# The row of f_j by two small transfers through DRAM in place of four transposes

## The chip, the cores and the metric

The kernel runs on one core of a Trainium2 chip. The metric is the device time of one execution in microseconds (us); the kernel before takes 2719.64 us in the median of three runs (2719.47 to 2719.93). A core has five engines with a queue of instructions each: TensorE (PE, matrix products and transposes; its weight loads are shown as PEld), VectorE (DVE), ScalarE (ACT), GpSimd (POOL) and SyncE (SP, which here only issues transfers). Each works through its own queue in order.

## The reference, cut to what matters

There are 128 graphs of 128 nodes with 256 features, in float32. One gated graph layer comes first, three graph attention layers follow; each is added to its input and normalised.

```python
# layer 0, three steps:  m = h @ weight[i];  aggr = A.T @ m;  h = gru_cell(aggr, h)
#   r, z = sigmoid(i + h);  n = tanh(i_n + r * h_n);  h = (1 - z) * n + z * h
x = layernorm(x + gated(x, adj, ...))
# layers 1, 2, 3:
Wh = x @ W.T
f_i, f_j = Wh @ a1, Wh @ a2
e = f_i[:, :, None] + f_j[:, None, :]
e = where(e > 0, e, 0.2 * e);  e = where(adj == 0, -large, e)
x = layernorm(x + softmax(e, axis=2) @ Wh)
```

The change is about `f_j[:, None, :]`: f_j is one number for each node, and each row i of the scores needs all 128 of them side by side.

## The kernel before, in words

**Tiling.** Nodes lie on the 128 partitions. Graphs go in 32 groups of four (`G = 4`), so that a tile is 128 x 512 (four graphs x 128) or 128 x 1024 (four graphs x 256 features). Each group has two phases: `gru`, the gated layer in three steps, and `gat`, three attention layers.

**The gated phase.** A step aggregates with the adjacency (L498), then multiplies in a two-by-two block scheme with seven products where eight are usual: `product` (L446) on PE writes to PSUM "gate" banks, `add` (L451) on DVE joins parts, ACT applies tanh (L524, L553), DVE and GpSimd form the new state (L540 to L563), and PE transposes it (L579). In the last step the group's x, loaded once more (L569), is added (L582).

**The attention phase.** The scores need f_i and f_j, each a product-sum of a node's features with a vector; L605 makes eight of them on DVE per layer (four graphs for f_j first, then four for f_i), each writing the product itself to a junk tile `fx`. f_j then stands in one column, one node per partition. To get it as a row on all partitions, PE transposes the column, broadcast to 128 x 128, once for each graph (L614), into a PSUM bank. L619 on DVE adds the mask to that row and takes the row's maximum; ACT adds f_i and applies the slope (L623), and takes exp (L640); PE transposes the result (L647), multiplies it with the features (L663) and with the weights (L674); DVE scales and adds the residual (L680). `layernorm` squares on ACT (L389), takes the root on GpSimd (L392, L396) and scales on ACT (L402), from the tile `y` into another tile `xn`.

**What sets the order.** The program is written out in full as a list of operations with what they read and write, and class `Plan` orders them before anything is built. It plays the operations against its own clock: each has an assumed duration for each engine that could do it (for instance 440 ns for four transposes), a result can be used by another engine after `LATENCY` of the engine that made it (4000 ns for a transfer from SP), plus `lag` where an operation states one, and plus `MARGIN` (500 ns) before PE may use it. Among what is ready, the older group goes first; for the last four groups (`LAST = 4`) the stage counts instead, so that these four advance side by side. An operation may start only if a slot is free for each tile that it begins to fill: `pools` gives the number of slots for each kind (26 of "k2", 2 KB per partition; 19 of "k4", 4 KB; 3 PSUM "bank"s and 5 "gate"s), and `own` keeps some back for the oldest group. `port=BOTH` says that DVE and GpSimd may not run it beside each other's such operation. Each engine then runs its instructions in the order found, whatever the real times are; only semaphores hold an instruction back.

**Transfers.** SP issues them in plan order in one queue: `xs` (x of the group, L478), `adj_i` (adjacency as int32, L479), `y` (x again, L569) and the output (L687), each once per group. The int32 adjacency is turned into `am` (float 0 or 1, L483), and later into the additive mask (L570).

Of the kernel before, what the change touches and what calls it, by code (L numbers as in the profile page):

```python
# [23 lines left out]
FAR = -5.0 * 2.0 ** 97  # L24
# [23 lines left out]
class Plan:  # L48
# [2 lines left out]

    LATENCY = {"PE": 250, "ACT": 220, "DVE": 200, "POOL": 250, "SP": 4000}

    MARGIN = 500

# [140 lines left out]
def adj_resnorm_kernel(  # L198
# [14 lines left out]
    nc = tc.nc  # L213
    B = x.shape[0]
    NG = B // G
    LAST = 4

    consts = ctx.enter_context(tc.tile_pool(name="consts", bufs=1))
    work = ctx.enter_context(tc.tile_pool(name="work", bufs=1))
    psum = ctx.enter_context(tc.tile_pool(name="psum", bufs=1, space=bass.MemoryType.PSUM))  # L220


    pools = {"gru": 4, "xs": 2, "adj": 2, "am": 5, "k2": 26, "k4": 19, "fx": 2, "f": 3, "mv": 4, "st": 6, "v": 16,
             "gate": 5, "bank": 3}
    own = ({"k2": 8, "k4": 5, "gate": 2, "v": 5, "fx": 0, "st": 0}, {"k2": 4, "k4": 2, "v": 5, "fx": 0, "st": 0})
    floats = {"gru": 0, "k4": 1024, "xs": 1024, "fx": 256, "f": 8, "mv": 8, "st": 6, "v": 4}
# [3 lines left out]
    slots = {t: [(psum if t in ("gate", "bank") else work).tile([P, w], I32 if t == "adj" else F32, name=f"{t}{i}")  # L230
                 for i in range(n)] for t, (n, w) in tags.items() if w}

    def T(b):
        if b.at is None:
            width = 1
            for s in b.shape:
                width *= s
            at = slots[b.tag][b.slot][:, 0:width]
            if len(b.shape) == 2:
                at = at.rearrange("p (a b) -> p a b", b=b.shape[-1])  # L240
            elif len(b.shape) == 3:
                at = at.rearrange("p (a b c) -> p a b c", b=b.shape[-2], c=b.shape[-1])
            b.at = at
        return b.at

    def bank():
        return Buf("bank", GN)
# [7 lines left out]
    ident = consts.tile([P, P], F32)  # L255
# [111 lines left out]
            res.append(dst)  # L367
        return res

    def layernorm(y, total, dst, prio):  # L370

        rstd, ve, shift = Buf("v", G), Buf("v", G), Buf("v", G)
        if total is None:
            mv = Buf("mv", G, 2)
            for b in range(G):
                st = Buf("st", 6)
                plan.op({"DVE": 400}, lambda e, b=b, st=st: nc.vector.bn_stats(T(st), T(y)[:, b, :]),
                        reads=[(y, b)], writes=[st], prio=prio)
                plan.op({"DVE": 95}, lambda e, b=b, st=st: nc.vector.bn_aggr(T(mv)[:, b, :], T(st)),
                        reads=[st], writes=[(mv, b)], prio=prio)  # L380
            plan.op({"POOL": 229}, lambda e: nc.gpsimd.tensor_scalar(T(ve), T(mv)[:, :, 1], EPS, None, op0=ALU.add),
                    reads=[(mv, b) for b in range(G)], writes=[ve], prio=prio)
            less, keys = (lambda: T(mv)[:, :, 0]), [(mv, b) for b in range(G)]
        else:
            mean, ss = Buf("v", G), Buf("v", G)
            plan.op({"DVE": 100}, lambda e: nc.vector.tensor_scalar(T(mean), T(total), -1.0 / D, None, op0=ALU.mult),  # L386
                    reads=[(total, b) for b in range(G)], writes=[mean], prio=prio)
            for b in range(G):
                plan.op({"ACT": 490}, lambda e, b=b: nc.scalar.activation(  # L389
                    T(dst)[:, b, :], T(y)[:, b, :], AF.Square, bias=T(mean)[:, b:b + 1], accum_out=T(ss)[:, b:b + 1]),  # L390
                    reads=[(y, b), mean], writes=[(dst, b), (ss, b)], prio=prio)
            plan.op({"POOL": 229}, lambda e: nc.gpsimd.tensor_scalar(  # L392
                T(ve), T(ss), 1.0 / D, EPS, op0=ALU.mult, op1=ALU.add),
                reads=[(ss, b) for b in range(G)], writes=[ve], prio=prio)
            less, keys = (lambda: T(mean)), [mean]
        plan.op({"POOL": 1035}, lambda e: nc.gpsimd.tensor_tensor(T(rstd), T(ve), neghalf, ALU.pow),  # L396
                reads=[ve], writes=[rstd], prio=prio)
        plan.op({"DVE": 100}, lambda e: nc.vector.scalar_tensor_tensor(  # L398
            T(shift), less(), -1.0 if total is None else 1.0, T(rstd), op0=ALU.mult, op1=ALU.mult),
            reads=keys + [rstd], writes=[shift], prio=prio)  # L400
        for b in range(G):
            plan.op({"ACT": 500}, lambda e, b=b: nc.scalar.activation(  # L402
                T(dst)[:, b, :], T(y)[:, b, :], AF.Identity, bias=T(shift)[:, b:b + 1], scale=T(rstd)[:, b:b + 1]),
                reads=[(y, b), shift, rstd], writes=[(dst, b)], prio=prio)

    def sums(ms, prio):

# [63 lines left out]

    def gru(g, stage):

        xs, adj_i, am = Buf("xs", G, D), Buf("adj", G, P), Buf("am", G, P)
        prio = stage(g, 0)
        turn = Buf("gru")
        x_g = x[g * G:(g + 1) * G].rearrange("b n d -> n b d")
        plan.op({"SP": 60}, lambda e: nc.sync.dma_start(T(xs), x_g), writes=[xs], prio=prio)  # L478
        plan.op({"SP": 60}, lambda e: nc.sync.dma_start(T(adj_i), adj[g * G:(g + 1) * G].rearrange("b s t -> s b t")),  # L479
                writes=[adj_i], prio=prio)  # L480
        if g == 0:
            hidden_weights(prio)
        plan.op({"DVE": 417}, lambda e: nc.vector.tensor_scalar(T(am), T(adj_i), 0, None, op0=ALU.not_equal),  # L483
                reads=[adj_i], writes=[am, turn], prio=prio, port=BOTH)
        hT = transposed(xs, lambda b, c: T(xs)[:, b, c * P:(c + 1) * P], prio)
        h = None
        for i in range(STEPS):
            prio = stage(g, i)
            if g == 0:
                input_weights(i, prio)  # L490
            agg = []
            for c in range(KC):
                b_, a_ = bank(), Buf("k2", GN)
# [23 lines left out]
            nn = strassen([(2, (h_in,)), (2, (a_in,))], halves, prio)  # L517
            hT2 = []
            for c in range(KC):

                o, v, d = rz[c], nn[c], Buf("k2", GN)
# [44 lines left out]
                hT2.append(d)  # L566
            if last:
                y = Buf("k4", G, D)
                plan.op({"SP": 60}, lambda e: nc.sync.dma_start(T(y), x_g), reads=[agg[0]], writes=[y], prio=prio)  # L569
                plan.op({"DVE": 417}, lambda e: nc.vector.tensor_scalar(  # L570
                    T(am), T(am), 0.0, FAR, op0=ALU.is_equal, op1=ALU.mult), reads=[am], writes=[am], prio=prio, port=BOTH)
            else:
                h2 = [Buf("k2", G, P) for c in range(KC)]
# [17 lines left out]
        x1 = Buf("k4", G, D)  # L591
        layernorm(y, None, x1, prio)
        return x1, am

    def gat(g, xc, no, stage):

        for l in range(3):
# [9 lines left out]
                        accum_out=T(f)[:, b, h:h + 1]), reads=[(xc, b), (wa, l)], writes=[fx, (f, 2 * b + h)], prio=prio, port=BOTH)  # L607
            e_, pT, y = Buf("k2", G, P), Buf("k2", G, P), Buf("k4", G, D)
            top, nmax, den, rden, total = Buf("v", G), Buf("v", G), Buf("v", G), Buf("v", G), Buf("v", G)
            b_ = bank()  # L610

            def fn(e, b_=b_, f=f):
                for b in range(G):
                    nc.tensor.transpose(T(b_)[:, b * P:(b + 1) * P],  # L614
                                        T(f)[:, b, 1:2].to_broadcast([P, P]), ident)
            plan.op({"PE": 440}, fn, reads=[(f, 2 * b + 1) for b in range(G)], writes=[b_], prio=prio)

            for b in range(G):
                plan.op({"DVE": 215}, lambda e, b_=b_, b=b, e_=e_, top=top: nc.vector.tensor_tensor_reduce(  # L619
                    T(e_)[:, b, :], T(b_)[:, b * P:(b + 1) * P], T(no)[:, b, :], 1.0, 3 * FAR, ALU.add, ALU.max,  # L620
                    T(top)[:, b:b + 1]), reads=[b_, no], writes=[(e_, b), (top, b)], prio=prio)
            for b in range(G):
                plan.op({"ACT": 285}, lambda e, b=b, f=f, e_=e_: nc.scalar.activation(  # L623
                    T(e_)[:, b, :], T(e_)[:, b, :], AF.Prelu, bias=T(f)[:, b, 0:1], alpha=SLOPE),
# [43 lines left out]
            for b0 in range(0, G, 2):  # L668
# [9 lines left out]
                for b in (b0, b0 + 1):  # L678
# [5 lines left out]
            xn = Buf("k4", G, D)  # L684
            layernorm(y, total, xn, prio)
            xc = xn
# [57 lines left out]
```

## Time and profile before

| | |
|---|---|
| time, median of 3 | 2719.64 us (2719.47 to 2719.93) |
| span of the profiled run | 2716.7 us |
| PE / weight loads / DVE / ACT / GpSimd busy | 98 / 87 / 75 / 65 / 22% |
| L614, four transposes per layer and group | 384 transposes |
| L619, scores from the PSUM row | 384, 284 ns each on DVE |
| L605, sums for f | 768, 436 ns each on DVE |
| DMA packets, bytes | 70106, 65.39 MB |

How to read it: durations overlap, [...] so what an instruction costs its engine is the distance between two starts. A float32 product is recorded on PE as two MATMUL records, a transpose as one. The line of digits gives 40 equal slices of the span in tenths. "a <- b" in a wait means that a sat idle until b released it.

### The profile page before, as it was taken

Reading aid. Unit: us, or ns where it says so; the run is one execution under the profiler, and the core shown is the slowest. Engines: PE = TensorE matmul, PEld = TensorE weight load, DVE = VectorE, ACT = ScalarE, POOL = GpSimd, SP = SyncE. Lnnn points to the kernel's source line nnn. Section 1 sums busy time; section 2 is a strip of 40 time slices with the busy share of each in tenths; the row PEclk is TensorE's granted clock in tenths of the full one; section 3 lists DMA queues with packets and bytes.
Section 4 is the critical chain, followed back from the end, with each engine's and each line's share of the span. In section 5 each row is a group of like instructions: output and inputs, shape, how many; then the busy total and the mean of one; then the engine's idle time right before and its main releaser. Section 6 shows DMA issues by size and latency. Waiting matters only on the chain.

```text
span 2716.7 us, 42471 instructions
## 1 busy us (share of the span) xinstructions
PE 2660.0 (98%) x14536; PEld 2366.2 (87%) x14536; DVE 2026.1 (75%) x6206; ACT 1760.2 (65%) x4632; POOL 593.0 (22%) x738
## 2 busy tenths in 40 slices
PE   7999999999999999999999999999999999999987
PEld 6888889888888888888888888988988888888875
DVE  4677777787787776777876777877777877776696
ACT  3566666666666666666767666666676666665577
POOL 1013222211131222122221222212222312222021
PEclk9999999999999999999999999999999999999999
DMA  3001000000010100001000000100000000000000
GB/s 120 9 20 36 28 5 24 28 28 20 13 33 12 36 20 20 16 20 36 20 28 28 9 28 20 36 20 20 17 20 28 28 24 21 9 9 27 13 1 32
DMA packets 70106, 65.39 MB, mean 24 GB/s; under 512 B 2688, under 2 KB 68224, under 8 KB 69888
## 3 DMA queue, kind: packets, MB, share of 16 engines
q1 hardware_dynamic: 67584, 58.73, 7.1%
q10 hardware_dynamic: 2304, 3.95, 0.4%
q8 instruction: 114, 1.87, 0.3%
q14 instruction: 104, 0.85, 0.1%
HBM read 45.89 MB, written 16.78 MB: 23 GB/s over the span
## 4 chain that ended last, share of the span: by engine, by line
PE 86%; DVE 8%; ACT 3%; issue 1%; DMA 1%; POOL 0%; POOLq 0%; ACTq 0%; SPq 0%; DVEq 0%
PE gate L446 58%; PE bank L674 10%; PE bank L663 6%; PE bank L498 5%; PE bank L579 3%; DVE fx L605 2%; PE bank L647 1%; DVE k L451 1%; PE bank L614 1%; ACT k L402 1%; ACT k L389 1%; DVE k L680 1%; DVE k L286 1%; PE bank L333 1%; DVE k L540 1%
## 5 line engine op out<-in xcount | busy, mean ns | idle before, releaser
L446 PE MATMUL gate<-k,whs 128*128 128x256 f32 x4032 | 1202.2, 380 | 3.0 <-ACT k L513 2.2
L446 PE MATMUL gate<-k,wcs 128*128 128x256 f32 x4032 | 1199.2, 379 | 0.0
L446 PEld LDWEIGHTS gate<-k,wcs 128*128 128x128 f32 x4032 | 766.1, 190 | 104.0
L446 PEld LDWEIGHTS gate<-k,whs 128*128 128x128 f32 x4032 | 728.5, 190 | 86.2 <-ACT k L513 3.4
L451 DVE TENSOR_TENSOR k<-gate,k 128x512 f32<-128x512 f32 x576 | 390.4, 686 | 264.3 <-PE gate L446 220.9
L284 ACT COPY k<-bank 128x512 f32<-128x512 f32 (+1 forms) x459 | 262.3, 583 | 191.7 <-PE bank L579 62.7
L674 PE MATMUL bank<-gwT,k 128*128 128x256 f32 x1536 | 352.6, 382 | 5.0 <-DVE k L286 3.5
L416 POOL TENSOR_TENSOR k<-k,k 128x256 f32<-128x256 f32 x302 | 248.9, 841 | 402.0 <-DVE k L563 133.9
L674 PEld LDWEIGHTS bank<-gwT,k 128*128 128x128 f32 x1536 | 290.6, 191 | 49.7 <-DVE k L286 8.6
L605 DVE SCALAR_TENSOR_TENSOR fx<-k,wa 128x256 f32<-128x256 f32 x768 | 290.3, 436 | 51.2 <-ACT k L402 49.4
L389 ACT ACTIVATE k<-k,v 128x256 f32<-128x256 f32 x384 | 190.3, 498 | 210.6 <-DVE v L386 210.2
L402 ACT ACTIVATE k<-k,v,v 128x256 f32<-128x256 f32 x512 | 263.7, 593 | 54.7 <-DVE v L398 54.4
L524 ACT ACTIVATE k<-k,brz 128x512 f32<-128x512 f32 (+1 forms) x384 | 226.1, 619 | 80.6 <-DVE k L451 80.2
L680 DVE SCALAR_TENSOR_TENSOR k<-bank,v,k 128x256 f32<-128x256 f32 x384 | 169.9, 480 | 119.9 <-PE bank L674 119.3
L506 ACT COPY k<-gate 128x512 f32<-128x512 f32 x288 | 164.7, 580 | 109.8 <-PE gate L446 108.6
L553 ACT ACTIVATE k<-k,bi 128x512 f32<-128x512 f32 x192 | 137.8, 722 | 108.5 <-DVE k L550 71.1
L663 PEld LDWEIGHTS bank<-k,k 128*128 128x128 f32 x1536 | 185.9, 192 | 14.2 <-DVE k L286 5.3
L663 PE MATMUL bank<-k,k 128*128 128x128 f32 x1536 | 188.2, 275 | 7.8 <-DVE k L286 4.7
L558 POOL TENSOR_TENSOR k<-k,k 128x512 f32<-128x512 f32 x78 | 103.3, 1327 | 412.3 <-ACT k L553 406.1
L286 DVE COPY k<-bank 128x512 f32<-128x512 f32 x225 | 152.9, 685 | 49.3 <-PE bank L579 17.4
L392 POOL TENSOR_SCALAR v<-v 128x4 f32<-128x4 f32 x96 | 20.5, 214 | 773.4 <-ACT k L389 749.9
L510 ACT ACTIVATE k<-gate,bhn 128x256 f32<-128x256 f32 x288 | 135.5, 470 | 46.7 <-PE gate L446 45.9
(79 smaller groups left out, 3116.0 us busy)
## 6 DMA issues: line engine op xcount, KB each, us to landing
xs<-in_x_dram SPq DMA_DIRECT2D x32, 512.0 KB, 3.9
k<-in_x_dram SPq DMA_DIRECT2D x32, 512.0 KB, 4.0
out_dram<-k SPq DMA_DIRECT2D x32, 512.0 KB, 3.0
adj<-in_adj_dram SPq DMA_DIRECT2D x32, 256.0 KB, 2.9
k<-in_w_hhT_dram ACTq DMA_DIRECT2D x2, 384.0 KB, 6.6
k<-in_w_ihT_dram ACTq DMA_DIRECT2D x2, 384.0 KB, 6.5
k<-in_gnn_wT_dram ACTq DMA_DIRECT2D x3, 256.0 KB, 5.6
k<-in_gat_w_dram ACTq DMA_DIRECT2D x3, 256.0 KB, 5.2
```

The lines of the kernel that those rows point to most:

```text
L284: nc.scalar.copy(dst, src)
L286: nc.vector.tensor_copy(dst, src)
L389: plan.op({"ACT": 490}, lambda e, b=b: nc.scalar.activation(T(dst)[:, b, :], T(y)[:, b, :], AF.Square, bias=T(mean)[:, b:b + 1], accum_out ...
L402: plan.op({"ACT": 500}, lambda e, b=b: nc.scalar.activation(T(dst)[:, b, :], T(y)[:, b, :], AF.Identity, bias=T(shift)[:, b:b + 1], scale= ...
L416: nc.vector if e == "DVE" else nc.gpsimd).tensor_tensor(T(t)[:, j, :], a(), b(), ALU.subtract),
L446: nc.tensor.matmul(T(dst)[:, j * H:(j + 1) * H], T(w)[:, m, gt, :], moving(m, ms)[1](), start=first and n == 0, stop=n == len(todo) - 1, s ...
L451: plan.op({"DVE": 630}, lambda e: nc.vector.tensor_add(T(o)[:, :, j * H:(j + 1) * H], T(b_).rearrange("p (g n) -> p g n", g=2), T(part).re ...
L524: nc.scalar.activation(T(o)[:, gt, n0:n1], src(), AF.Tanh, bias=brz[:, gt * KC + c:gt * KC + c + 1], scale=0.5)
L605: plan.op({"DVE": 345}, lambda e, b=b, h=h, l=l, f=f, fx=fx, xc=xc: nc.vector.scalar_tensor_tensor(T(fx), T(xc)[:, b, :], 1.0, T(wa)[:, l, ...
L663: nc.tensor.matmul(T(b_)[:, b * P:(b + 1) * P], T(xc)[:, b, c * P:(c + 1) * P], T(pT)[:, b, :], start=True, stop=True)
L674: nc.tensor.matmul(T(b_)[:, (b - b0) * D:(b - b0 + 1) * D], T(aT[k])[:, b * P:(b + 1) * P], T(gwT)[:, l, k, :], start=(k == 0), stop=(k == ...
L680: nc.vector.scalar_tensor_tensor(T(y)[:, b, :], T(b_)[:, (b - b0) * D:(b - b0 + 1) * D], T(rden)[:, b:b + 1], T(xc)[:, b, :], op0=ALU.mult ...
```

## The change

The row of f_j no longer comes from PE. For all groups but the last four, SP writes column f_j of the four graphs (128 partitions x 4 floats) into a small DRAM tile `row` and reads this back, broadcast to all 128 partitions, straight into the score tile `e_`, where the score instruction works in place. The last four groups keep the transposes. The purpose is to take those instructions off PE. To let the planner place the waiting, transfers get landing times of their own (`LATENCY` of SP 2500 ns plus a `lag` for each kind). Around it, tiles are saved: the int32 adjacency is loaded into `am` itself and converted in place (6 slots of `am` for 5 and 2 of `adj`), layernorm works in place on `y` with a junk tile `jx` for the squares, `fx` has one slot instead of two; and `y` is loaded later, after the first tanh of the last step.

```diff
-    LATENCY = {"PE": 250, "ACT": 220, "DVE": 200, "POOL": 250, "SP": 4000}
+    LATENCY = {"PE": 250, "ACT": 220, "DVE": 200, "POOL": 250, "SP": 2500}
...
-    pools = {"gru": 4, "xs": 2, "adj": 2, "am": 5, "k2": 26, "k4": 19, "fx": 2, "f": 3, "mv": 4, "st": 6, "v": 16,
+    pools = {"gru": 4, "xs": 2, "am": 6, "k2": 26, "k4": 19, "fx": 1, "jx": 1, "f": 3, "row": 3, "mv": 4, "st": 6, "v": 16,
...
+    slots["row"] = [dram.tile([G, P], F32, name=f"row{i}") for i in range(pools["row"])]
...
-                    T(dst)[:, b, :], T(y)[:, b, :], AF.Square, bias=T(mean)[:, b:b + 1], accum_out=T(ss)[:, b:b + 1]),
-                    reads=[(y, b), mean], writes=[(dst, b), (ss, b)], prio=prio)
+                    T(jx), T(y)[:, b, :], AF.Square, bias=T(mean)[:, b:b + 1], accum_out=T(ss)[:, b:b + 1]),
+                    reads=[(y, b), mean], writes=[jx, (ss, b)], prio=prio)
...
-                T(dst)[:, b, :], T(y)[:, b, :], AF.Identity, bias=T(shift)[:, b:b + 1], scale=T(rstd)[:, b:b + 1]),
-                reads=[(y, b), shift, rstd], writes=[(dst, b)], prio=prio)
+                T(y)[:, b, :], T(y)[:, b, :], AF.Identity, bias=T(shift)[:, b:b + 1], scale=T(rstd)[:, b:b + 1]),
+                reads=[(y, b), shift, rstd], writes=[(y, b)], prio=prio)
...
-        plan.op({"SP": 60}, lambda e: nc.sync.dma_start(T(xs), x_g), writes=[xs], prio=prio)
-        plan.op({"SP": 60}, lambda e: nc.sync.dma_start(T(adj_i), adj[g * G:(g + 1) * G].rearrange("b s t -> s b t")),
-                writes=[adj_i], prio=prio)
+        plan.op({"SP": 60}, lambda e: nc.sync.dma_start(T(xs), x_g), writes=[xs], prio=prio, lag=1500)
+        plan.op({"SP": 60}, lambda e: nc.sync.dma_start(T(am).bitcast(I32), adj[g * G:(g + 1) * G].rearrange("b s t -> s b t")),
+                writes=[am], prio=prio, lag=500)
...
-                plan.op({"SP": 60}, lambda e: nc.sync.dma_start(T(y), x_g), reads=[agg[0]], writes=[y], prio=prio)
+                plan.op({"SP": 60}, lambda e: nc.sync.dma_start(T(y), x_g), reads=[(nn[0], 5)], writes=[y], prio=prio, lag=1500)
...
-            b_ = bank()
-
-            def fn(e, b_=b_, f=f):
-                for b in range(G):
-                    nc.tensor.transpose(T(b_)[:, b * P:(b + 1) * P],
-                                        T(f)[:, b, 1:2].to_broadcast([P, P]), ident)
-            plan.op({"PE": 440}, fn, reads=[(f, 2 * b + 1) for b in range(G)], writes=[b_], prio=prio)
+
+            if g < NG - LAST:
+                row = Buf("row", P)
+                plan.op({"SP": 60}, lambda e, row=row, f=f: nc.sync.dma_start(
+                    slots["row"][row.slot].rearrange("b n -> n b"), T(f)[:, :, 1]),
+                    reads=[(f, 2 * b + 1) for b in range(G)], writes=[row], prio=prio, lag=6500)
+                plan.op({"SP": 60}, lambda e, row=row, e_=e_: nc.sync.dma_start(
+                    T(e_).rearrange("p b j -> p (b j)"),
+                    slots["row"][row.slot].rearrange("b n -> (b n)").partition_broadcast(P)),
+                    reads=[row], writes=[(e_, b) for b in range(G)], prio=prio, lag=1900)
+                rows, keys, port = (lambda b, e_=e_: T(e_)[:, b, :]), lambda b: [], BOTH
+            else:
...
-                plan.op({"DVE": 215}, lambda e, b_=b_, b=b, e_=e_, top=top: nc.vector.tensor_tensor_reduce(
-                    T(e_)[:, b, :], T(b_)[:, b * P:(b + 1) * P], T(no)[:, b, :], 1.0, 3 * FAR, ALU.add, ALU.max,
-                    T(top)[:, b:b + 1]), reads=[b_, no], writes=[(e_, b), (top, b)], prio=prio)
+                plan.op({"DVE": 215}, lambda e, rows=rows, b=b, e_=e_, top=top: nc.vector.tensor_tensor_reduce(
+                    T(e_)[:, b, :], rows(b), T(no)[:, b, :], 1.0, 3 * FAR, ALU.add, ALU.max,
+                    T(top)[:, b:b + 1]), reads=keys(b) + [no, (e_, b)], writes=[(e_, b), (top, b)], prio=prio, port=port)
```

More of the change, by code (lines that the diff above doesn't have):

```diff
@@ L219, in adj_resnorm_kernel @@
     work = ctx.enter_context(tc.tile_pool(name="work", bufs=1))
+    dram = ctx.enter_context(tc.tile_pool(name="dram", bufs=1, space=bass.MemoryType.DRAM))
     psum = ctx.enter_context(tc.tile_pool(name="psum", bufs=1, space=bass.MemoryType.PSUM))
-    pools = {"gru": 4, "xs": 2, "adj": 2, "am": 5, "k2": 26, "k4": 19, "fx": 2, "f": 3, "mv": 4, "st": 6, "v": 16,
+    pools = {"gru": 4, "xs": 2, "am": 6, "k2": 26, "k4": 19, "fx": 1, "jx": 1, "f": 3, "row": 3, "mv": 4, "st": 6, "v": 16,
              "gate": 5, "bank": 3}
-    own = ({"k2": 8, "k4": 5, "gate": 2, "v": 5, "fx": 0, "st": 0}, {"k2": 4, "k4": 2, "v": 5, "fx": 0, "st": 0})
-    floats = {"gru": 0, "k4": 1024, "xs": 1024, "fx": 256, "f": 8, "mv": 8, "st": 6, "v": 4}
+    own = ({"k2": 8, "k4": 5, "gate": 2, "v": 5, "fx": 0, "jx": 0, "st": 0}, {"k2": 4, "k4": 2, "v": 5, "fx": 0, "jx": 0, "st": 0})
+    floats = {"gru": 0, "k4": 1024, "xs": 1024, "fx": 256, "jx": 256, "f": 8, "mv": 8, "st": 6, "v": 4}
     tags = {t: (n, floats.get(t, 512)) for t, n in pools.items()}
@@ L229, in adj_resnorm_kernel @@
     plan = Plan({t: n for t, (n, _) in tags.items()}, own)
-    slots = {t: [(psum if t in ("gate", "bank") else work).tile([P, w], I32 if t == "adj" else F32, name=f"{t}{i}")
-                 for i in range(n)] for t, (n, w) in tags.items() if w}
+    slots = {t: [(psum if t in ("gate", "bank") else work).tile([P, w], F32, name=f"{t}{i}")
+                 for i in range(n)] for t, (n, w) in tags.items() if w and t != "row"}
+    slots["row"] = [dram.tile([G, P], F32, name=f"row{i}") for i in range(pools["row"])]
     def T(b):
@@ L368, in transposed, with layernorm @@
         return res
-    def layernorm(y, total, dst, prio):
+    def layernorm(y, total, prio):
         rstd, ve, shift = Buf("v", G), Buf("v", G), Buf("v", G)
@@ L388, in layernorm @@
             for b in range(G):
-                plan.op({"ACT": 490}, lambda e, b=b: nc.scalar.activation(
-                    T(dst)[:, b, :], T(y)[:, b, :], AF.Square, bias=T(mean)[:, b:b + 1], accum_out=T(ss)[:, b:b + 1]),
-                    reads=[(y, b), mean], writes=[(dst, b), (ss, b)], prio=prio)
+                jx = Buf("jx", D)
+                plan.op({"ACT": 490}, lambda e, b=b, jx=jx: nc.scalar.activation(
+                    T(jx), T(y)[:, b, :], AF.Square, bias=T(mean)[:, b:b + 1], accum_out=T(ss)[:, b:b + 1]),
+                    reads=[(y, b), mean], writes=[jx, (ss, b)], prio=prio)
             plan.op({"POOL": 229}, lambda e: nc.gpsimd.tensor_scalar(
@@ L472, in gru @@
     def gru(g, stage):
-        xs, adj_i, am = Buf("xs", G, D), Buf("adj", G, P), Buf("am", G, P)
+        xs, am = Buf("xs", G, D), Buf("am", G, P)
         prio = stage(g, 0)
@@ L477, in gru @@
         x_g = x[g * G:(g + 1) * G].rearrange("b n d -> n b d")
-        plan.op({"SP": 60}, lambda e: nc.sync.dma_start(T(xs), x_g), writes=[xs], prio=prio)
-        plan.op({"SP": 60}, lambda e: nc.sync.dma_start(T(adj_i), adj[g * G:(g + 1) * G].rearrange("b s t -> s b t")),
-                writes=[adj_i], prio=prio)
+        plan.op({"SP": 60}, lambda e: nc.sync.dma_start(T(xs), x_g), writes=[xs], prio=prio, lag=1500)
+        plan.op({"SP": 60}, lambda e: nc.sync.dma_start(T(am).bitcast(I32), adj[g * G:(g + 1) * G].rearrange("b s t -> s b t")),
+                writes=[am], prio=prio, lag=500)
         if g == 0:
             hidden_weights(prio)
-        plan.op({"DVE": 417}, lambda e: nc.vector.tensor_scalar(T(am), T(adj_i), 0, None, op0=ALU.not_equal),
-                reads=[adj_i], writes=[am, turn], prio=prio, port=BOTH)
+        plan.op({"DVE": 417}, lambda e: nc.vector.tensor_scalar(T(am), T(am).bitcast(I32), 0, None, op0=ALU.not_equal),
+                reads=[am], writes=[am, turn], prio=prio, port=BOTH)
         hT = transposed(xs, lambda b, c: T(xs)[:, b, c * P:(c + 1) * P], prio)
@@ L590, in gru @@
                 h, hT = h2, hT2
-        x1 = Buf("k4", G, D)
-        layernorm(y, None, x1, prio)
-        return x1, am
+        layernorm(y, None, prio)
+        return y, am
     def gat(g, xc, no, stage):
@@ L609, in gat, with fn @@
             top, nmax, den, rden, total = Buf("v", G), Buf("v", G), Buf("v", G), Buf("v", G), Buf("v", G)
-            b_ = bank()
-            def fn(e, b_=b_, f=f):
-                for b in range(G):
-                    nc.tensor.transpose(T(b_)[:, b * P:(b + 1) * P],
-                                        T(f)[:, b, 1:2].to_broadcast([P, P]), ident)
-            plan.op({"PE": 440}, fn, reads=[(f, 2 * b + 1) for b in range(G)], writes=[b_], prio=prio)
+            if g < NG - LAST:
[9 more added lines that the diff above has]
+            else:
+                b_ = bank()
+                def fn(e, b_=b_, f=f):
+                    for b in range(G):
+                        nc.tensor.transpose(T(b_)[:, b * P:(b + 1) * P],
+                                            T(f)[:, b, 1:2].to_broadcast([P, P]), ident)
+                plan.op({"PE": 440}, fn, reads=[(f, 2 * b + 1) for b in range(G)], writes=[b_], prio=prio)
+                rows, keys, port = (lambda b, b_=b_: T(b_)[:, b * P:(b + 1) * P]), lambda b, b_=b_: [b_], ("POOL",)
@@ L683, in gat @@
                             reads=[b_, rden, (xc, b)], writes=[(y, b), (total, b)], prio=prio)
-            xn = Buf("k4", G, D)
-            layernorm(y, total, xn, prio)
-            xc = xn
+            layernorm(y, total, prio)
+            xc = y
         plan.op({"SP": 60}, lambda e: nc.sync.dma_start(out[g * G:(g + 1) * G].rearrange("b n d -> n b d"), T(xc)),
```

## The prediction, made before the changed kernel had run

> **What bounds the kernel now.** I read the shares of the engines first, then stretches of time, then the chain of work that ended last. The page's first two parts:
>
> ```profile
> PE 2660.0 (98%) x14536; PEld 2366.2 (87%) x14536; DVE 2026.1 (75%) x6206; ACT 1760.2 (65%) x4632; POOL 593.0 (22%) x738
> PE   7999999999999999999999999999999999999987
> PEclk9999999999999999999999999999999999999999
> ```
>
> TensorE (PE) has work all the time and its clock is full; VectorE (DVE) is at 75%. The same by stretches (columns: length, busy time and count of each engine, clock, DMA share, GB/s):
>
> ```profile
> core 0: us, PE busy (x) PEld busy (x) DVE busy (x) ACT busy (x) POOL busy (x), PEclk, DMA share, GB/s
> 0.00:35.00 35.00, 18.81 (x81) 15.16 (x82) 11.51 (x31) 9.84 (x18) 5.09 (x12) 1.00 0.68 218
> 35.00:400.00 365.00, 362.87 (x1955) 321.60 (x1954) 256.02 (x691) 216.95 (x535) 80.56 (x88) 1.00 0.06 19
> 400.00:2400.00 2000.00, 1989.11 (x10957) 1778.93 (x10956) 1527.90 (x4683) 1327.34 (x3507) 452.32 (x567) 1.00 0.08 23
> 2400.00:2600.00 200.00, 198.87 (x1037) 175.85 (x1037) 138.56 (x338) 111.93 (x267) 34.65 (x41) 1.00 0.05 14
> 2600.00:2717.00 117.00, 90.33 (x512) 74.68 (x510) 92.11 (x466) 94.10 (x308) 20.39 (x30) 0.96 0.06 19
> ```
>
> PE is idle for 16 us in the head, 27 us in the tail and for only 14 us in all the 2,565 us between. So in the middle, where the change acts, a PE instruction taken away shortens the run, unless PE then waits for something else. The chain says the same:
>
> ```profile
> PE gate L446 58%; PE bank L674 10%; PE bank L663 6%; PE bank L498 5%; PE bank L579 3%; DVE fx L605 2%; PE bank L647 1%; DVE k L451 1%; PE bank L614 1%; ACT k L402 1%; ACT k L389 1%; DVE k L680 1%; DVE k L286 1%; PE bank L333 1%; DVE k L540 1%
> ```
>
> L614, the four transposes that spread f_j, stands in it as 1%. What they cost is read from the PE timeline, by start times, since the durations overlap:
>
> ```profile
> 1323.81 0.59 PE L446 MATMUL gate<-k,wcs 128*128 128x256 f32 x2
> 1324.25 0.60 PE L614 MATMUL bank<-ident,f 128*128 128x128 f32 x4
> 1324.68 0.60 PE L446 MATMUL gate<-k,whs 128*128 128x256 f32 x2
> ...
> 1337.27 3.62 PE L674 MATMUL bank<-gwT,k 128*128 128x256 f32 x16
> ...
> 1352.09 0.60 PE L614 MATMUL bank<-ident,f 128*128 128x128 f32 x4
> ...
> 1358.58 0.60 PE L647 MATMUL bank<-ident,k 128*128 128x128 f32 x4
> ```
>
> Four transposes hold PE for 1324.68 - 1324.25 = 0.43 us, as much as one gate product. The later lines give one attention layer's latency: from the end of the last layer's output product (1337.27 + 3.62 = 1340.9) over layernorm, f, scores and exp to the transposes of the weights (1358.6) it is 17.7 us; over the 81 layers between 200 and 2430 us the median is 17.6 and the fastest tenth 15.4 or less. During this time PE does gate products of the next group of graphs.
>
> For the new transfers the nearest rows are the DMA issues (count, KB of each, us from issue to landing), with the load queue's packets:
>
> ```profile
> xs<-in_x_dram SPq DMA_DIRECT2D x32, 512.0 KB, 3.9
> k<-in_x_dram SPq DMA_DIRECT2D x32, 512.0 KB, 4.0
> adj<-in_adj_dram SPq DMA_DIRECT2D x32, 256.0 KB, 2.9
> bi<-in_b_ih_dram ACTq DMA_DIRECT2D x1, 3.0 KB, 2.7
> q1 hardware_dynamic: 67584, 58.73, 7.1%
> ```
>
> Even 3 KB take 2.7 us to land, and the 16 DMA engines are 7% busy.
>
> **What the Trainium skill says.** "Perfetto Trace Analysis", Identifying the Most-Contended Engine, warns that matmul busy time overstates how full PE is and asks for the weight loads' share: here 87%. So I cost by start-to-start pitch. The sum of all pitches (4032 + 768 products of 0.432 us, each in the profile as two records, 1,536 narrow ones of 0.222, also two records each, 1,792 transposes of 0.108, weights 20) is 2,628 us of 2,717: the bound holds. "DMA: Bandwidth & Descriptors", Rules for kernel authors: a strided last dimension makes one descriptor per element, and a DMA that reads what another wrote must wait for its completion semaphore. No run here shows either; the second means two full landings in a row. The same page, Anatomy of one DMA, puts about 2 us fixed cost on a DMA, most of it the write receipt; the 2.7 us of the 3 KB load agree.
>
> **The change part by part.**
>
> *Removed from PE.* 28 of 32 groups x 3 layers = 84 sets x 0.43 us = 36.3 us (the last four groups keep theirs). In a stretch 99.5% busy this is on the path: 2719.6 - 36.3 = 2683.3.
>
> *Added latency.* In its place: a write of f[:, :, 1], 128 partitions x 4 single floats, to DRAM, then a read of that 2 KB row into all partitions (256 KB). The trace shows neither. The write: from below 2.7 us (the 3 KB load). From above: one descriptor for each of 512 floats, 32 on each of 16 engines, at 0.2 us each if every one pays the HBM access the DMA page gives (Latency and other measured facts), 6.4 us, on top of 2.7: 9.1, an estimate. The planner of the changed kernel assumes 2.5 + 6.5 = 9.0. The read: from below 2.9 (the 256 KB adjacency load), from above 4.4, what the planner assumes. For loads that I can compare, the planner's new figures are 4.0, 3.0 and 4.0 against 3.9, 2.9 and 4.0 in the trace, so I take the upper values, 9.0 + 4.4 = 13.4; both ends, 5.6 and 13.5, stay for the range.
>
> *Is it hidden?* The orders of instructions of the changed kernel tell how much other work is put in the gap. On DVE, between the fourth product that makes f_j and the first score instruction, there are 4 to 14 us of other instructions, 10.7 us in the mean (at the durations of the trace); at DVE's 76% share in the middle this is 14.0 us of time, just over 13.4. On PE, from a layer's last output product to the next layer's weight transposes, there are 28.2 us of work in the mean (22 to 31). The chain needs 17.6 - 1.0 (from the transposes to the first score, which goes) + 13.4 = 30.0 at the median pace, or 15.4 - 1.0 + 13.4 = 27.8 at the pace of the fastest tenth. So it is hidden when the chain goes briskly, with nothing to spare. To fill PE two groups' attention phases are now interleaved (f_j buffers of two groups alternate), where before one followed another at a 27 us pitch.
>
> *The SyncE queue.* 168 small transfers join 128 large ones in one queue, in order. The read waits for its row's landing, and whatever stands behind it waits too. In 65 of 84 cases nothing stands between write and read; in 19 a large transfer (2.9 to 4.0 us) does and can push the read back. I take 1 us each, half reaching PE: 19 x 0.5 = 9.5, say 8 us in all, because DVE is idle a quarter of the time and absorbs some. Score instructions behind a late row hold up all of DVE, gate additions (L451) included, and through the gate banks PE: that is how lateness would show.
>
> *DVE, ACT, GpSimd.* Scores now read SBUF: 336 x about 65 ns less ("Perfetto Trace Analysis", Optimizing Scalar/DVE Operations: 60 against 125 ns access) = -22 us of DVE. The planner moves 101 subtractions from GpSimd to DVE (471 for 370): 101 x 0.45 = +45. One junk buffer for f products instead of two makes each wait for its neighbour: pitch 0.35 becomes at most 0.47, 768 x 0.12 = +92 at most. DVE stays below 2026 + 115 = 2141, 80%: no bound. In the middle all this costs nothing, since PE's queue is the full one. In the tail, where the chain runs over DVE and ACT, one chain has 24 such products (+2.9 us) and 12 squares sharing one junk tile (pitch 0.52 to about 0.68, +1.9), part of it beside the other three groups: +3 us.
>
> *Memory.* In-place layernorm frees a large buffer per layer, and the adjacency is converted in place, with six buffers: these make room for the second attention phase. In the head two more 256 KB loads come early; at the head's rate of about 360 GB/s 1.4 us, taken as +1.
>
> Sum: 2683.3 + 8 + 1 + 3 = 2695.
>
> **The rivals.** *More than the transposes* (0.12): row lands in 5.6 us in all, nothing waits, and the freed buffers also take some 10 us from the 41 us idle in middle and tail: 2673. For it: the lower bounds. Against: the tail's chain is latency. *Gain mostly eaten* (0.15): the 1.8 us by which 30.0 exceeds 28.2 show on PE in a fifth of their size, 84 x 0.36 = 30 us: 2719.6 - 36.3 + 30 = 2713. *The wait takes the transposes' place* (0.17): half of 1.8 us on each of 84 layers, 76 us: 2759, slower. For it: queues in order cannot step past a late row, and the budget is even. Against: two groups and gate products of a third are at hand, and DVE has a quarter free.
>
> **How the numbers follow.** Forecast 0.56, at 2695. The range goes from 2674 (leaving half the best case out) to 2730 (leaving the slow case out). Faster: forecast, best case and half of the eaten one, 0.76; within 0.2% 0.08; slower 0.16.
>
> **What will show it.** Right: no L614 in the middle, PE still over 99% busy there, waits of DVE's score line on the row of a few tens of us in all, f write landing near 9 us and the row near 4. Wrong: waits of score instructions or gate additions of over a hundred us, PE idle in the middle of more than 40 us, y loads arriving after their transposes, or a tail longer by 10 us.

## The result, and the profile after

| | before | changed |
|---|---|---|
| time, median | 2719.78 us (2719.47 to 2719.98) | 3064.47 us (3058.31 to 3071.34) |
| ratio, 95% interval | | 1.127 (1.125 to 1.129) |
| span of the profiled run | 2716.7 us | 3056.4 us |

The change makes the kernel 345 us slower. The forecast was 2695 us, with a range to 2730.

The page of the changed kernel, with its engines, its slices and its load queue:

```profile
PE 2740.4 (90%) x14200; PEld 2398.4 (78%) x14200; DVE 2060.1 (67%) x6308; ACT 1773.2 (58%) x4620; POOL 527.0 (17%) x648
PE   7998898989898988898898989889899889989987
PEclk9999999999999999998999989989999999999989
q1 hardware_dynamic: 124032, 80.93, 11.9%
```

The 336 transposes have gone (14536 - 14200), and yet PE has 80 us more of busy time; it is idle for 316 us of its span, where it was idle for 57. The mean clock over the run is 0.954 of full speed, before 0.998. The same in the middle and at the end (stretch, length, busy time and count of each engine, clock, DMA share, GB/s):

```profile
core 0: us, PE busy (x) PEld busy (x) DVE busy (x) ACT busy (x) POOL busy (x), PEclk, DMA share, GB/s
400.00:2400.00 2000.00, 1795.81 (x9313) 1573.23 (x9312) 1351.87 (x4155) 1165.64 (x3046) 356.25 (x436) 0.95 0.14 29
2935.00:3057.00 122.00, 91.08 (x509) 76.52 (x507) 94.65 (x473) 97.83 (x319) 19.82 (x30) 0.90 0.05 18
```

In 2,000 us of the middle PE is idle for 204 us where it was 11. The tail, 6.6 us longer (116.0 us for 109.4 from the end of the last gate product to the end of the run), is not where the time went. No other engine has become full either: DVE is at 67%. So everybody waits for something that is no engine. The chain of work that ended last names it:

```profile
PE 48%; DMA 31%; DVE 9%; ACT 8%; issue 2%; POOL 1%; SPq 0%; ACTq 0%; DVEq 0%; POOLq 0%
PE gate L449 28%; DMA row<-f 18%; DMA k<-row 12%; PE bank L689 8%; PE bank L678 4%; PE bank L501 3%; DVE fx L607 2%; ACT k L405 2%; PE bank L582 2%; ACT k L655 2%; DVE k L634 1%; ACT k L638 1%; DVE k L454 1%; PE bank L662 1%; ACT jx L392 1%
```

The write of the row (L615) and its reading back (L618) are 30% of the chain; gate products fell from 58% to 28%. The waits (engine, tile and line, released by; us in all, times, longest):

```profile
ACT k L638 <- DVE v L634: 374.0, 78, 13.4
DVE k L634 <- DMA k<-row: 372.2, 69, 13.8
PE bank L662 <- ACT k L655: 81.9, 23, 10.5
PE gate L449 <- DVE k L454: 75.1, 24, 7.9
```

DVE's score instruction L634 sits idle 372 us for its row, and the rest of the list reads as the same delay passed on: the slope on ACT (L638) waits for the score, the weight transposes on PE (L662) wait for the exp (L655), and gate products wait for the gate additions (L454), which stand behind the score in DVE's queue. Last, how long the two transfers take, us from issue to landing, first of L615 and then of L618 (the trace gives the landing of 73 of the 84 writes and 56 of the 84 reads):

```profile
DMA to landing us min/median/max: 8.7/10.8/16.9
DMA to landing us min/median/max: 3.2/4.5/15.3
```

The planner had placed them at 9.0 and 4.4. That is nearly the fastest write, not the usual one. The medians make 15.3 us against 13.4 planned, and by the DMA packets none of the 84 rows was there in less than 13.8 us; the longest of each is more than 6 us beyond.

One such case, from the chain (start, duration in us):

```profile
1357.19 10.98 DMA row<-f
1368.17 0.02 issue
1368.18 14.28 DMA k<-row
1382.46 0.02 issue
1382.49 0.29 DVE k L634
```

A read that lands in 4.5 us as a rule took 14.28. At 1362.4 the second group under way had issued its own write, which took 16.2 us; the read had that write's 512 single floats ahead of it or beside it. Eight of the 84 reads were issued while another group's write was under way; they took 12 to 15 us, and 100 of the 372 us of waiting are theirs. In the case above PE then had nothing left (start, duration; in brackets the idle time before it and its releaser):

```profile
1384.54 1.63 PE L662 MATMUL bank<-ident,k 128*128 128x128 f32 x4 [10.54 <-ACT k L655]
1386.30 1.22 PE L449 MATMUL gate<-k,whs 128*128 128x256 f32 x2
1387.32 1.06 PE L449 MATMUL gate<-k,wcs 128*128 128x256 f32 x2
1388.17 1.06 PE L449 MATMUL gate<-k,whs 128*128 128x256 f32 x2
1389.03 0.98 PE L449 MATMUL gate<-k,wcs 128*128 128x256 f32 x2
1389.85 0.60 PE L449 MATMUL gate<-k,whs 128*128 128x256 f32 x2
1390.28 0.59 PE L449 MATMUL gate<-k,wcs 128*128 128x256 f32 x2
```

PE stood for 10.54 us, and for some 5 us after it the products start 0.82 to 1.02 us apart (1388.17 - 1387.32 = 0.85); then 0.43 again. So a pause costs more than its own length. The Trainium skill describes it: "TensorE: Matmul & The Clock Gate", Part 1, has PE at half clock after an idle window of about 3.4 us, and at full clock again after as long a time of work. The trace agrees in kind, with some 5 us here (1384.54 to 1389.85).

### The profile page after: what moved, and what is told of

Read it like the earlier page. It is cut to its first block, busy times and chain, and to the rows that moved or that the text cites. A ratio compares the mean times of both kernels' runs of the same rounds, so it can differ in the third digit from the quotient of the medians.

```text
span 3056.4 us, 42155 instructions
## 1 busy us (share of the span) xinstructions
PE 2740.4 (90%) x14200; PEld 2398.4 (78%) x14200; DVE 2060.1 (67%) x6308; ACT 1773.2 (58%) x4620; POOL 527.0 (17%) x648
## 3 DMA queue, kind: packets, MB, share of 16 engines
q1 hardware_dynamic: 124032, 80.93, 11.9%
## 4 chain that ended last, share of the span: by engine, by line
PE 48%; DMA 31%; DVE 9%; ACT 8%; issue 2%; POOL 1%; SPq 0%; ACTq 0%; DVEq 0%; POOLq 0%
PE gate L449 28%; DMA row<-f 18%; DMA k<-row 12%; PE bank L689 8%; PE bank L678 4%; PE bank L501 3%; DVE fx L607 2%; ACT k L405 2%; PE bank L582 2%; ACT k L655 2%; DVE k L634 1%; ACT k L638 1%; DVE k L454 1%; PE bank L662 1%; ACT jx L392 1%
## 5 line engine op out<-in xcount | busy, mean ns | idle before, releaser
L449 PE MATMUL gate<-k,whs 128*128 128x256 f32 x4032 | 1237.7, 389 | 134.5 <-DVE k L454 75.1
L449 PE MATMUL gate<-k,wcs 128*128 128x256 f32 x4032 | 1225.5, 386 | 0.0
L449 PEld LDWEIGHTS gate<-k,whs 128*128 128x128 f32 x4032 | 757.3, 195 | 245.1 <-DVE k L454 83.4
L449 PEld LDWEIGHTS gate<-k,wcs 128*128 128x128 f32 x4032 | 784.0, 194 | 112.2
L454 DVE TENSOR_TENSOR k<-gate,k 128x512 f32<-128x512 f32 x576 | 391.6, 687 | 231.7 <-PE gate L449 157.1
L607 DVE SCALAR_TENSOR_TENSOR fx<-k,wa 128x256 f32<-128x256 f32 x768 | 329.5, 429 | 51.2 <-ACT k L405 32.9
L638 ACT ACTIVATE k<-k,f 128x128 f32<-128x128 f32 x384 | 125.2, 391 | 374.0 <-DVE v L634 374.0
L689 PEld LDWEIGHTS bank<-gwT,k 128*128 128x128 f32 x1536 | 291.6, 193 | 56.1 <-ACT k L286 11.6
L634 DVE CUSTOM_DVE_ANT_0 k<-k,am 128x128 f32<-128x128 f32 x336 | 82.3, 299 | 372.3 <-DMA k<-row 372.2
L527 ACT ACTIVATE k<-k,brz 128x256 f32<-128x256 f32 (+1 forms) x384 | 226.9, 619 | 108.6 <-DVE k L454 108.4
L419 POOL TENSOR_TENSOR k<-k,k 128x256 f32<-128x256 f32 x213 | 177.0, 842 | 414.2 <-ACT k L286 215.4
L392 ACT ACTIVATE jx<-k,v 128x256 f32<-128x256 f32 x384 | 194.7, 507 | 52.4 <-DVE v L388 44.4
L678 PEld LDWEIGHTS bank<-k,k 128*128 128x128 f32 x1536 | 187.6, 194 | 16.9 <-DVE k L288 7.4
## 6 DMA issues: line engine op xcount, KB each, us to landing
row<-f SPq DMA_DIRECT2D x84, 2.0 KB, 10.8
```

What stands on the lines that cost most here:

```text
L392: plan.op({"ACT": 490}, lambda e, b=b, jx=jx: nc.scalar.activation(T(jx), T(y)[:, b, :], AF.Square, bias=T(mean)[:, b:b + 1], accum_out=T( ...
L419: nc.vector if e == "DVE" else nc.gpsimd).tensor_tensor(T(t)[:, j, :], a(), b(), ALU.subtract),
L449: nc.tensor.matmul(T(dst)[:, j * H:(j + 1) * H], T(w)[:, m, gt, :], moving(m, ms)[1](), start=first and n == 0, stop=n == len(todo) - 1, s ...
L454: plan.op({"DVE": 630}, lambda e: nc.vector.tensor_add(T(o)[:, :, j * H:(j + 1) * H], T(b_).rearrange("p (g n) -> p g n", g=2), T(part).re ...
L527: nc.scalar.activation(T(o)[:, gt, n0:n1], src(), AF.Tanh, bias=brz[:, gt * KC + c:gt * KC + c + 1], scale=0.5)
L607: plan.op({"DVE": 345}, lambda e, b=b, h=h, l=l, f=f, fx=fx, xc=xc: nc.vector.scalar_tensor_tensor(T(fx), T(xc)[:, b, :], 1.0, T(wa)[:, l, ...
```

## The experiments

The theory after this reading, *late rows*: the landings are longer than planned, DVE stands in its fixed order until each row is there, and PE runs dry. Rivals: *the order* (the planner's new order, the shared tiles, the later loads cost the time, whatever the row does) and *traffic* (the transfers load the queue and delay the loads that everybody needs). All ratios are to the kernel before.

### The other edits alone

All groups keep their transposes; buffers, in-place layernorm and landing times are those of the change.

```diff
-            if g < NG - LAST:
+            if False:
```

> All edits of the change, but every group keeps the four transposes and no row goes through DRAM. Theory 'late rows' (the score instructions wait for rows that land later than the order allows; the other edits cost nothing): 2700 to 2730 us, DVE waits for a row gone. Rival 'order' (two attention phases interleaved, single junk tiles, in-place layernorm make the order itself poor): clearly above 2730.

2721.67 us, 1.0006 (0.9998 to 1.0015), in the range named for *late rows*. The other edits together cost nothing and bring nothing, in the order that the planner finds for them. What is lost is lost with the row. In this kernel the int32 adjacency lands 2.8 us after its issue. Loads are waited for in the first 40 us of the run only, `xs` like this:

```profile
PE bank L366 <- DMA xs<-in_x_dram: 5.2, 1, 5.2
```

### The transfers without anyone waiting

The kernel of the first experiment, but both transfers are issued as in the change; the read goes to a tile `sc` that nothing uses. Apart from SP, the order of instructions is the same as in the first experiment.

```diff
+                row, sc = Buf("row", P), Buf("sc", GN)
...
-                    T(e_).rearrange("p b j -> p (b j)"),
+                    T(sc),
...
-            else:
+            if True:
```

> All groups keep the transposes; the two transfers are issued as well, at the places the planner gives them, but the read goes to a scratch tile that nobody uses. It measures the traffic without the wait. Theory 'late rows': within 15 us of the run with transposes alone, 2700 to 2745. Rival 'contention': over 2800.

2755.74 us, 1.0136 (1.012 to 1.0153): 34.1 us more than without the transfers, and 11 us above the range named for *late rows*. The landings of the loads and the waits for them, on the page and in the waits of this kernel:

```profile
xs<-in_x_dram SPq DMA_DIRECT2D x32, 512.0 KB, 5.0
am<-in_adj_dram SPq DMA_DIRECT2D x32, 256.0 KB, 9.0
```

```profile
DVE k L585 <- DMA k<-in_x_dram: 30.6, 9, 6.6
PE bank L366 <- DMA xs<-in_x_dram: 15.3, 5, 5.0
```

Traffic alone delays the adjacency to 9.0 us for 2.8 (the trace gives 3 of its 32 landings; by the packets of all 32, the last one ends 8.1 us after the issue, for 2.5) and makes DVE wait for `y` (L585). So this rival is real, but with 34 us it is a tenth of the loss. In the changed kernel, whose adjacency lands in 3.0 us, the waits for these loads after the first 40 us come to 4.3 us, beside the 372 for the row.

### The same row in pieces of 16 bytes, same order

This takes the lateness away and leaves plan and order of the changed kernel as they are. `f` is laid out so that the four graphs' f_j of one node lie side by side: the write has 128 pieces of 16 bytes for 512 of 4. The row then arrives with the graphs interleaved, and somebody must read it with a stride of 16 bytes.

```diff
-            f = Buf("f", G, 2)
+            f = Buf("f", 2, G)
...
-    slots["row"] = [dram.tile([G, P], F32, name=f"row{i}") for i in range(pools["row"])]
+    slots["row"] = [dram.tile([P, G], F32, name=f"row{i}") for i in range(pools["row"])]
...
-                    slots["row"][row.slot].rearrange("b n -> n b"), T(f)[:, :, 1]),
+                    slots["row"][row.slot], T(f)[:, 1, :]),
...
-                    slots["row"][row.slot].rearrange("b n -> (b n)").partition_broadcast(P)),
+                    slots["row"][row.slot].rearrange("n b -> (n b)").partition_broadcast(P)),
```

In the first form the whole score tile `e_` stays interleaved, for every pass from score to weight transposes.

> The same plan and order as the changed kernel, but f_j of the four graphs lies side by side, so the write is 128 pieces of 16 bytes instead of 512 of 4, and the score tile is read with a stride. Theory 'late rows': the write lands in about 4.5 us instead of 10.8, in all under the 13.4 us that the order allows, waits of the score line on the row fall from 372 us to under 30, and the time comes to 2680 to 2710. Rival 'order': stays above 2900, since the order is the same. Rival 'contention' (the 256 KB reads load the rings): 2800 to 2950.

2742.5 us, 1.0083 (1.0068 to 1.0098). This is 32 us above the range named for *late rows* and far below both rivals. The write lands in 1.4 us in place of 10.8, and DVE waits for the row once, for 2.2 us. The strided passes are slower, though: a slope or exp on ACT 511 ns for 391 to 393 before, a weight load of the transposes 197 ns for 141, a score 394 ns in the median and 452 in the mean for 299.

In the second form the row lands in a tile `raw` of its own. Only the score reads with a stride; it writes a dense `e_`:

```diff
-                row = Buf("row", P)
+                row, raw = Buf("row", P), Buf("k2", G, P)
...
-                rows, keys, port = (lambda b, e_=e_: T(e_)[:, b, :]), lambda b: [], BOTH
+                rows, keys, port = (lambda b, raw=raw: T(raw)[:, b, :]), lambda b, raw=raw: [raw], BOTH
```

> The 16-byte rows with the order of the changed kernel, but the row lands in a tile of its own; only the score instruction reads it with a stride, so that the two ScalarE passes and the transposes after it run over dense data again. Theory 'strided scores cost the rest' (ScalarE's passes at 511 ns for 391 make the order late): 2685 to 2710. Rival 'interleaved order cannot be kept full even with rows in time': within 10 us of 2742. If the transposes' 36 us come in whole: 2683.

2712.77 us, 0.9972 (0.996 to 0.9983), 3 us above the range named for strided scores. Page, waits and middle stretch of this kernel (its lines stand 3 or 4 lower, the score is L638):

```profile
PE 2635.7 (97%) x14200; PEld 2345.2 (87%) x14200; DVE 2100.6 (77%) x6308; ACT 1774.0 (65%) x4620; POOL 534.0 (20%) x648
q1 hardware_dynamic: 91776, 80.93, 11.3%
k<-row SPq DMA_DIRECT2D x84, 256.0 KB, 4.2
row<-f SPq DMA_DIRECT2D x84, 2.0 KB, 1.4
```

```profile
DVE k L638 <- DMA k<-row: 2.5, 3, 1.9
```

```profile
400.00:2400.00 2000.00, 1974.00 (x10739) 1762.75 (x10738) 1592.53 (x4779) 1343.84 (x3509) 416.53 (x506) 1.00 0.13 33
```

This decides. The order on every engine is that of the changed kernel, and as many bytes cross the same queue. The pieces are fewer (124032 - 91776 = 32256 packets = 84 x 384), the waits for the row fall from 372 to 2.5 us, and the time falls by 3064.5 - 2712.8 = 351.7 us, to less than before. The rival *order* has fallen for all but some 30 us, told below. The two profiles also divide the gap: PE is busy 105 us less for the same 14200 instructions (2740.4 - 2635.7) and idle 241 us less (316.0 - 75.0). The 105 us fit the slow clock after the pauses: the mean clock was 0.954 and is 0.992. An estimate comes near: the changed kernel's trace has 33 pauses of PE over 3.4 us, and half of the 5.3 us seen above, lost after each, makes 87 us.

### More time for the row

If lateness is the cause, a plan that allows 20 us (13.5 + 6.5) must help even with single floats. The same plan with 16 byte pieces tells what the allowance itself costs; but for SP the two have one order.

```diff
-                    reads=[(f, 2 * b + 1) for b in range(G)], writes=[row], prio=prio, lag=6500)
+                    reads=[(f, 2 * b + 1) for b in range(G)], writes=[row], prio=prio, lag=11000)
...
-                    reads=[row], writes=[(e_, b) for b in range(G)], prio=prio, lag=1900)
+                    reads=[row], writes=[(e_, b) for b in range(G)], prio=prio, lag=4000)
```

> The changed kernel with lags of 11000 and 4000 ns in place of 6500 and 1900, so that the planner allows 20 us for write and read. Theory 'late rows': most rows then land in time, 2690 to 2800, the rest being pairs of rows in flight together. Rival 'order': above 2950. A mixed theory (not enough other work to fill 20 us): 2800 to 2950 with waits on the row gone but TensorE idle.

2821.2 us, 1.0372 (1.0357 to 1.0388). This is 21 us above the range named for *late rows*; the range of the mixed theory holds it, but the waits on the row are not gone. The score's wait in this kernel:

```profile
DVE k L634 <- DMA k<-row: 63.4, 15, 6.4
```

> The 16-byte rows with a tile of their own and the planner told 20 us for write and read, as in the run with long lags. That run took 2821 us with only 63 us of waits on the row. If its loss came from the single-float writes standing in the way of other transfers: this one comes to 2700 to 2730, like the run with 13.4 us. If 20 us are more than the other work can fill: 2780 to 2830.

2740.49 us, 1.0075 (1.006 to 1.009), between the two ranges named. So 6.6 us more of allowance take 243 us off the changed kernel (3064.5 - 2821.2), far more than any two orders with rows in time differ here: the loss was lateness. But waiting longer on purpose is no cure. With 16 byte pieces the plan with the long allowance, which has another order, is 28 us slower than the one with 13.4 us (2740.5 against 2712.8), and 80.7 us still come from the single floats (2821.2 - 2740.5), for a row that is still late 15 times and for loads that land behind the pieces (PE waits 25.7 us for `xs` in 7 cases).

### One row at a time

With one DRAM tile for the rows in place of three, the next write can't be issued until the last row has been read. This takes the pairs of writes away, and is planned anew.

```diff
-"row": 3
+"row": 1
```

> The changed kernel with one DRAM row tile instead of three, so that no second write of single floats is in flight before the first row has been read. If pairs of writes in flight make the late rows: landing of the read at most 7 us, waits of the score line on the row fall from 372 to about 150 us and the time to 2800 to 2900. If each row alone is late by the same: above 2950.

2998.73 us, 1.1027 (1.1004 to 1.105). The longest write is now 11.5 us for 16.9 and the longest read 6.4 for 15.3 (of the 18 writes and 21 reads whose landing the trace gives; the packets of all 84 reads end no later), so pairs do make the extremes. But the kernel is only 66 us faster, as named for rows that are each late alone. The waits of this kernel:

```profile
DVE k L634 <- DMA k<-row: 211.1, 66, 7.1
DVE am L486 <- DMA am<-in_adj_dram: 86.9, 15, 9.7
PE bank L366 <- DMA xs<-in_x_dram: 35.3, 6, 9.4
```

Nearly every row still takes longer by itself than the 13.4 us planned: by the packets, 83 of 84 do, with 14.1 us in the median. And SP, held up longer, brings the other loads late. Pairs are a part of it, the single floats the root.

### A tight plan and a fitted one

With 16 byte pieces, the allowance can be cut to what was measured, 1.7 + 4.5 = 6.2 us, with no reserve (second form above, `lag` -800 and 2000).

> The same with the planner told what the 16-byte row takes by the trace: 1.7 us for the write, 4.5 us for the read, 6.2 in place of 13.4. If landing times that fit are what counts: 2680 to 2705 and not slower than the run with the long allowance. Rival (an allowance with reserve is better, since rows land up to 2 us late): 5 to 30 us slower than that run.

2757.59 us, 1.0143 (1.0129 to 1.0157): 45 us slower than with 13.4 us allowed, which is more than either range named. The waits of this kernel:

```profile
DVE k L638 <- DMA k<-row: 80.0, 71, 3.3
ACT k L642 <- DVE v L638: 142.9, 92, 6.2
```

Here 71 of 84 rows are late, by 1.1 us each, though the read lands in 3.0 to 5.1 us. How much of the 45 us is this lateness and how much the new order was not separated. The last kernel allows 4.5 + 6.5 = 11 us, puts the strided score at 315 ns for 215, lets the load of `y` land 1.2 us later, and gives the junk tile `fx` its second slot back; the diff, in fragments of lines, is against the second form.

```diff
-writes=[row], prio=prio, lag=6500)
+writes=[row], prio=prio, lag=2000)
...
-reads=[row], writes=[raw], prio=prio, lag=1900)
+reads=[row], writes=[raw], prio=prio, lag=4000)
...
-{"DVE": 215}
+{"DVE": 315}
...
-"fx": 1
+"fx": 2
...
-writes=[y], prio=prio, lag=1500)
+writes=[y], prio=prio, lag=2700)
```

> The 16-byte rows with a tile of their own, allowances of 4.5 us for the write and 6.5 us for the read (measured 1.4 to 3.4 and 3.0 to 5.9), 5.2 us for the late load of x, the strided score instruction at its measured pitch of 315 ns, and two junk tiles for the f products again. If the planner's numbers, fitted with a reserve, are what the change lacked: 2680 to 2705, ahead of the kernel before. If the new order is moved by chance more than by the fit: 2700 to 2740.

2694.83 us, 0.9908 (0.9891 to 0.9924): faster than both kernels, by 25 us against before, and in the range named for a fitted plan. Its page and its middle stretch:

```profile
PE 2627.8 (98%) x14200; PEld 2342.6 (87%) x14200; DVE 2086.5 (77%) x6312; ACT 1761.9 (65%) x4600; POOL 537.0 (20%) x664
```

```profile
400.00:2400.00 2000.00, 1985.31 (x10813) 1779.38 (x10812) 1583.73 (x4773) 1336.17 (x3490) 420.25 (x517) 1.00 0.13 32
```

PE is idle for 15 us of the 2,000. Which of the four changes of this last kernel brought how much was not separated. Every new allowance gives a new order. The four plans with 16 byte pieces and dense scores lie between 2694.8 and 2757.6 us, so a difference of a per cent between two plans is not to be put down to one number in them.

## Why the prediction was wrong

*Removed from PE: right.* The sum began with 36.3 us off. The last experiment shows that it can be had in large part: PE is busy for 32.2 us less there (2660.0 - 2627.8), and the run is 25 us shorter, with the other edits of that kernel in it.

*Added latency: the sizes nearly right, their use wrong.* The write's upper estimate, 9.1 us, is close to the fastest landing, 8.7; I took it for the usual one, which is 10.8. The read was put at 4.4 and has a median of 4.5. The sum was thus 1.9 us short in the usual case.

*"Is it hidden?": the step that failed.* It found 13.4 us just inside the 14.0 us of DVE's gap, "hidden when the chain goes briskly, with nothing to spare", and went on as if a late row cost little. The gap was put too large, by even more than the latency was put too small. It can be read from the second form with 16 byte pieces, where the same order runs with the rows in time: by the starts in its trace, 11.6 us pass in the median from the issue of the write to the first score, and less than 13.4 us in 83 of 84 rows. One row of it:

```profile
1294.95 0.32 SPq L619 DMA_DIRECT2D row<-f  x1
1296.43 0.32 SPq L622 DMA_DIRECT2D k<-row  x1
1306.85 0.37 DVE L638 CUSTOM_DVE_ANT_0 k<-k,am 128x128 f32<-128x128 f32 x1
```

Here the gap is 1306.85 - 1294.95 = 11.9 us. The prediction's 10.7 us of other instructions are about the sum of their durations, in this trace 10.8 us in the mean. But durations overlap, and DVE is busy with these instructions for only 9.3 us. So even the 13.4 us assumed would not have fitted. With 15.3 us a row comes 3.7 us late as a rule, and the waits measured in the changed kernel are 372.2 / 84 = 4.4 us for each row.

*"The SyncE queue": the term that was mis-sized.* It counted what stands between a write and its own read in SP's order, 19 cases in 84, and put 8 us for all stalls, "because DVE is idle a quarter of the time and absorbs some". Measured by exchanging the pieces, with the strided scores that this brings, the stalls are 351.7 us, 4.2 us on each of 84 rows. Two things were missing. First, a transfer issued earlier by the *other* group can still be under way when the read is issued: the interleaving of two groups, which the prediction named as what fills PE, also brings two writes of single floats together. That is 100 of the 372 us; the other 272 are rows that are late without it. Second, idle time on DVE doesn't absorb a wait at the head of its queue: slope, exp, gate additions and then PE stand behind the score in one order written beforehand. Of 369.7 us less waiting of DVE, 241 came back as less idle time of PE; another 105 came from PE's faster instructions, by its clock as far as the estimate above goes. That DVE is idle a quarter of the time says that it has spare time, not that it has it at this place.

*The rival "The wait takes the transposes' place"* had the mechanism, "queues in order cannot step past a late row", with half of 1.8 us on each layer. The direction was that of the run; the size was 76 us and should have been 352, since a row was late by about 4 us and not by 1.8, more than half of it reached PE, and PE's clock fell besides. The sign of the forecast hung on that one size.

*Of the signs named beforehand* two hold: waits of score instructions over a hundred us (372), and PE idle in the middle for more than 40 us (204). The other two don't: the tail was longer by 6.6 us and not by 10, and `y` was waited for by 0.4 us in all.

*The rest, 2712.8 - 2683.3 = 29.5 us with the rows in time.* Head and tail had been put at +4. The profile of that kernel shows where to look, without a price for each: PE is idle for 26 us of 2,000 against 11, the mean clock is 0.992 for 0.998, strided scores start 0.31 us apart for 0.21, and `y` lands after 5.2 us where the plan has 4.0. "One junk buffer for f products" was expected to raise their pitch to at most 0.47 us; in that kernel 0.47 is the median and 0.54 occurs too, as here on DVE (1301.48 - 1300.94):

```profile
1300.94 0.42 DVE L610 SCALAR_TENSOR_TENSOR fx<-k,wa 128x256 f32<-128x256 f32 x1
1301.30 0.08 DVE L610 DVE_READ_ACCUMULATOR fx<-k,wa 128x1 f32 x1
1301.48 0.43 DVE L610 SCALAR_TENSOR_TENSOR fx<-k,wa 128x256 f32<-128x256 f32 x1
```

*Scores from SBUF: wrong, and of no weight.* I had expected 65 ns less for each, from what the Trainium skill states of access times in "Perfetto Trace Analysis", Optimizing Scalar/DVE Operations. Measured, a score takes 299 ns from SBUF and 284 from PSUM, and scores start 0.21 us apart in both.

*What stays open.* How much of the cost of traffic comes from SP, which issues in order and waits 718.6 us for written rows before their reads, and how much from DMA engines occupied with pieces, was not separated: a second issuing queue for the row was not tried.

## What to carry to other kernels

Before a short transfer goes into a latency that other work has to hide, count its contiguous pieces, not its bytes, and lay the source out so that pieces are as long as they can be; here a factor of four in the pieces was worth 352 us. Price the new latency under the traffic that the new order makes, with its spread, and compare the slow end with the gap. Measure the gap by starts, not by a sum of durations that overlap. On an engine that works through a fixed order, a wait at the head holds up all that stands behind it, however idle the engine is on average; here 241 of 370 us reached the engine that bounds the kernel, and that engine's clock fell on top. If gap and latency are about equal, "late by a little each time" is the forecast to work out first, and the number of times is what multiplies it.

## What the runs showed of the hardware

- A store of 2 KB from 128 partitions to DRAM lands in 10.8 us (median of the landings known) as 512 pieces of 4 bytes and in 1.4 us as 128 pieces of 16 bytes. With 16 DMA engines these are 24 more pieces for each; if they share them evenly, an estimate is (10.8 - 1.4) / 24 = 0.39 us a piece, where the prediction had taken 0.2. The 1.4 us are also below the 2.7 us of the 3 KB load, which the prediction took as the least for this write. The packet counts, 384 more for each write of single floats, agree with what the Trainium skill states in "DMA: Bandwidth & Descriptors", Rules for kernel authors: one descriptor for each element of a strided last dimension.
- Loads that have nothing to do with such a store can be late too when they share its queue: the adjacency 9.0 us for 2.8 with the transfers that nobody waits for, which took 34 us of run time. In the changed kernel it landed in 3.0.
- Reading f32 at a stride of 16 bytes costs: 511 ns for 391 in an ACT pass of 128x128, 0.31 us for 0.21 between DVE scores, 197 ns for 141 in a PE weight load.
- Accumulating instructions on DVE that write one shared junk tile start 0.46 to 0.54 us apart in the changed kernel, 0.47 in the median, and 0.35 with two tiles in the kernel before.
